# A graph layer on one core: fewer quads summed on TensorE, one-hot matrices ahead of the message product

## The chip, the cores and the metric

The kernel runs on one core of a Trainium2 chip. The core has four compute engines with a queue of instructions each: PE (TensorE, matrix products, with its weight loads in a row of their own, PEld), DVE (VectorE), ACT (ScalarE) and POOL (GpSimd). SP (SyncE) only issues DMAs here. The engines run side by side, each strictly in the order in which its instructions were written, and wait for each other by semaphores. The metric is the time of one execution in device microseconds (us), lower is better.

## The reference

6250 nodes with 128 features, 200000 edges. Each edge has a source and a target node (the edges come sorted by `dst`), 20 attributes and a weight. The layer normalises the node features, multiplies them by a matrix, makes a filter of 128 values for each edge from its attributes, multiplies the filter into the features of the edge's `dst` node, and sums the messages over the edge's `src` node, which is random:

```python
h = maximum(layernorm(x), 0)
xn = h @ W_in
W_ij = (softplus(f @ W_f1 + b_f1) - log 2) @ W_f2 + b_f2
W_ij = W_ij * edge_weight
out = segment_sum(xn[dst] * W_ij, src, 6250)
x + (softplus(out @ W_o1 + b_o1) - log 2) @ W_o2 + b_o2
```

All is in float32. The costly part is the sum into 6250 rows in random order.

## The kernel before

The edges are cut into chunks of 128 (one edge per partition), and four chunks make a quad: 391 quads. One loop (lines 1203 to 1248) has one pass, here called an item, per quad, and works on several quads at once, each one stage on: in item i the filter's first product `z` for quad i+1 (line 317) and its exponential and logarithm for quad i on ACT (322, 327); the gather of the node rows `xg` by a one-hot product (501) and the filter's second product `W` (509) for quad i-1; the scaling of `xg` by the edge weight on ACT into `xc` (514); and on DVE the message product, `W` times `xc` (524). `z`, `xg` and `W` share four PSUM banks in turn; a `z` takes the bank of the `W` three quads back, which the message product frees.

A quad's messages reach the sum in one of three ways, fixed by the quad's number:

- **Plain.** A product with an equality matrix sums the messages of a chunk that have the same source (536), and an indirect DMA from POOL adds the rows of the chunk to a table in DRAM (586): four scatters a quad, in item q+4. An equality matrix needs the sources broadcast to all partitions (loads at 348).
- **Listed.** Sixteen such quads make a window. Duplicated sources are found ahead of time (373 to 448), and get rows of their own in a list; the messages are scattered as they are, again four scatters a quad, in item q+2, and one more scatter a window adds the list. Of the plain and listed quads together 12 at the start and 19 at the end are plain.
- **Grouped.** The quad makes no scatter of its own. DVE builds a permutation matrix (`pm`, 665) that sorts the 512 edges into 16 groups of nodes with room for 32 edges each, and splits the message in a high part (ACT, 676) and a low or second part (DVE, 680) so that two passes of PE keep the precision. PE permutes (691, four outputs a quad), ACT copies the outputs out (696). Edges over 32 in a group go to a small overflow product (705, 706); two quads share one overflow, whose sums make one small scatter (`os`, `oji`). Eight grouped quads make a round. A round has four units, one for each of the permuted outputs: DVE builds a one-hot matrix for each quad (`so`, 768), PE multiplies (783, 64 products), DVE adds four PSUM banks to a sum in SBUF (794).

`sorted_quads` picks the grouped quads: it starts at `MP0` and steps by `MPGAPS`, over and over. Before, that is quad 2, then seven steps of 2 and one of 3: 8 of every 17 quads, 184 in all. `unit_slots` puts the units at offsets `UOFF` in that period.

The order of the rest is written out by hand. `at(item, point, function)` books a piece of work, and the loop runs the pieces of a point with `run`: `L` (loads, on SP), `D0` (first on DVE), `D1` (unit sums), `A0` and `A1` (on ACT ahead of the scaling), `DM` (DVE, just ahead of the message product), `PE2` (on PE behind the products of the item), `A2` (last on ACT), `D2` (last on DVE), `S` (scatters). `clear` moves a piece to a later item where a unit stands in its way. Node preparation (25 groups of 256 nodes, one every nine items: load, statistics, root, normalising, transpose, product, split in three parts, write of the table that `xg` is gathered from) and the split of the edge attributes run at such points too, so do the ranks in a group for eight quads at once (`rank_group` to `rank_slot`).

There are four tables for scatters. Two scatters into the same one must not overlap: the later one waits until the earlier one has landed. They are used in turn, the first two scatters into one table, then two, from the eighth three and from the 140th four. From a fixed scatter on one table gets no more and is added back within the loop (`r0_load`, `r0_tp`, `r0_add`).

Behind the loop all engines meet at a conditional loop (line 1277) that repairs rare cases and here does nothing. Then the tables are read (1360), added, and the output layer is computed in 13 groups.

The lines around the change in the loop:

```python
run(i, "A1")
if 0 <= i - 1 < NQ:
    s2_copy(i - 1)
run(i, "DM")
if 0 <= i - 1 < NQ:
    s2_m(i - 1)
```

Of the kernel before, what the change touches and what calls it, by code (L numbers as in the profile page):

```python
# [21 lines left out]
P = 128  # L22
# [15 lines left out]
LLATE = 16  # L38
# [16 lines left out]
def tile_gnn(ctx: ExitStack, tc: tile.TileContext, x, fB, cT, srcT, srcr, dstr, win_, wf1, wf2, bias, bo1c, wo1,  # L55
# [402 lines left out]
        mp["L", j] = {"so": idl[:, j:j + 1]}  # L458

    def l_dg(j):  # L460
        dg = wk.tile([P, P], F32, tag="h", name="ldg", bufs=1)
        nc.scalar.mul(dg, idt, idl[:, j:j + 1])
        mp["L", j]["dg"] = dg

    def l_same(j):
        eq = wk.tile([P, P], F32, tag="rm", name="leq", bufs=1)
# [371 lines left out]
    with tc.manual_schedule():  # L838
# [150 lines left out]
        for g in range(1, NG):  # L989
            if not spread:  # L990
                xt_load(g)
                for fn in (prep_stat, prep_rs0, prep_norm, prep_tp, prep_relu, prep_mm, prep_x1, prep_rm, prep_x2,
                           prep_x3):
                    fn(g)
                continue
            t0 = prep_start(g)
            at(t0 - 3, "L", xt_load, g)
            at(t0 - 1, "D2", prep_stat, g)
            at(t0, "A1", prep_rs0, g)
            at(t0, "D2", prep_norm, g)  # L1000
            at(t0 + 1, "PE2", prep_tp, g)
            at(t0 + 2, "A0", prep_relu, g)
            at(t0 + 2, "PE2", prep_mm, g)
            at(t0 + 3, "A0", prep_x1, g)
            at(t0 + 3, "DM", prep_rm, g)
            at(t0 + 3, "A2", prep_x2, g)
            at(t0 + 3, "D2", prep_x3, g)
        for b in range(1, NB):
            t0 = 2 if b == 1 else 8 * b - 8
            if b > 1:  # L1010
# [3 lines left out]
            at(t0 + 1, "A1", fb_3, b)  # L1014
            at(t0 + 1, "D2", fb_4, b)

        busy = units | {prep_start(g) + k for g in range(1, NG) for k in range(5)}
        mid = clear(NQ // 2, busy, 2) - 6 if spread else 0

        def late_loads():  # L1020
# [4 lines left out]

        def late_bias():
            nc.vector.tensor_scalar(nbo1, bo1_sb, -1.0, None, op0=ALU.mult)
            bb = wk.tile([P, 1, P], F32, tag="rm", name="bb", bufs=1)
# [6 lines left out]
            nc.vector.tensor_tensor(bo2b, bo2b, late["bps"][:, 0], op=ALU.add)  # L1035

        def bound_abs():
            t_ = wk.tile([K1, P], F32, tag="h", name="wabs", bufs=1)
            nc.scalar.activation(t_, w1f, AF.Abs)
            v_ = wk.tile([K1, P], F32, tag="rm", name="wsel", bufs=1)  # L1040
            nc.vector.tensor_copy(v_, con[:K1, 15:16].to_broadcast([K1, P]))
            late["wabs"] = t_, v_

# [62 lines left out]
            at(i, "PE2", r0_tp, g)  # L1106
            at(i + 1, "D0", r0_add, g)
        for r in range(-(-len(mpq) // RKQ)):
            i = max(mpq[RKQ * r], 5)
            at(i - 5, "D2", rank_group, r)  # L1110
            k = clear(i - 4, units)
            at(k, "PE2", rank_count, r)
            at(k + 1, "D0", rank_own, r)
            k = clear(k + 1, units)
            at(k, "PE2", rank_over, r)
            at(k + 1, "D0", rank_slot, r)
        for k in range(1, -(-NS // 2)):
            if not LB <= 2 * k < LE:
                at(max(0, splain[2 * k] - 2), "L", sb_load, k)
        for w in range((LE - LB) // SW):  # L1120
            for g in range(4):
                n = LB + SW * (w - 1) + 4 * g
                i = splain[n] + 2 if w else 6 + 2 * g
                for k in range(2):
                    kk = (LB + SW * w + 4 * g) // 2 + k
                    at(max(0, i + k - 2), "L", sb_load, kk)
                    at(i + k, "DM", l_eq, kk)
                i = clear(i + 2, units)
# [24 lines left out]
        if LE:  # L1153
            for k in range(NACC):
# [2 lines left out]
        for q in mpq:  # L1157
# [20 lines left out]
            if mpi[q] % 2 or q == mpq[-1]:  # L1178
                at(q + 5, "DM", over_idx, q)
                at(q + 6, "A0", over_dg, q)  # L1180
                k = clear(q + 6, units)
                at(k, "PE2", over_row, q)
                at(k + 1, "D0", over_eq, q)
                k = clear(q + 8, units)
# [15 lines left out]
        full = {-1: False}  # L1200
        r0_end = r0_at
        s1_pe(0)
        for i in range(max(NQ + 7, last + 16, r0_end + 2, lend + 24)):
            if i % 2 == 0 and i // 2 + 2 <= (NQ - 1) // 2:
                load_sc(i // 2 + 2)
            run(i, "L")
# [296 lines left out]
def base_caps(n, n_sc):  # L1503
    groups = node_groups(n)
    caps = []
    for s in range(n_sc):
        ready = n
        if big(n_sc) or s < 2:
            for g in range(1, len(groups)):
                if prep_start(g) + 3 >= 2 * s - 4:  # L1510
                    ready = groups[g][0]
                    break
        caps.append(ready - WIN)
# [86 lines left out]
```

## Time and profile before

| what | value |
|---|---|
| median of 3 runs | 2111.23 us (2109.82 to 2115.32) |
| profiled execution, its own time | 2102.09 us |
| its span | 2100.2 us |
| busy: PE, DVE, POOL, ACT | 85%, 84%, 76%, 73% |
| mean granted clock of PE | 0.93 |
| DMA | 269.16 MB, 128 GB/s |
| grouped quads, listed, plain | 184, 176, 31 |
| scatters of POOL: listed, plain, small | 704, 124, 103 |

The profiled execution is one run; its time stands 0.4% under the median of the three others. A row of a group gives the line, the engine, the operation, the output and the inputs, their shapes and the count; then the busy time in us and the mean length in ns; then the idle time that the engine had just ahead of these instructions and what ended it. A row of the waits gives who waited for whom, us in total, how often, and the longest. In a row by stretch stand the stretch, its length, the busy time of an engine with its count, the granted clock, the share of the DMA engines and GB/s.

### The profile page before, as it was taken

The page shows a single profiled execution, that of the slowest core. Times are in us where ns is not written, and L with a number is a line of the kernel's source. Part 1 is how long each engine was busy: PE and PEld are TensorE (multiplying, and loading weights), DVE is VectorE, ACT ScalarE, POOL GpSimd, SP SyncE. Part 2 cuts the span into 40 slices and gives each one's busy share as a digit, 9 for nine tenths or more (in the row PEclk, how much of TensorE's full clock was granted, in tenths as well). Part 3 has the DMA queues.
Part 4 walks back from the last instruction along what each step waited for, and adds up shares of the span by engine and source line. Part 5 has one row for each costly group of instructions (what it writes and reads, how often), then busy time and mean ns, then how long its engine had stood idle before and what let it go on. Part 6 is the DMA issues. An engine that isn't in the chain of part 4 may idle for free. (4 is left out here: it accounts for less than half of the span.)

```text
span 2100.2 us, 52738 instructions
## 1 busy us (share of the span) xinstructions
PE 1786.8 (85%) x17881; PEld 1532.4 (73%) x17881; DVE 1762.2 (84%) x4448; ACT 1537.2 (73%) x4392; POOL 1601.1 (76%) x984
## 2 busy tenths in 40 slices
PE   3579888887987898988988888888999899998966
PEld 2468777776776777877777777777777777887854
DVE  5687988898888898988989889798898888989865
ACT  3568777776776777777778687687877788898824
POOL 3557888786876877788787788788888888888844
PEclk9789999998999999989999999899999999999978
DMA  7886666665765666666676667666666666767649
GB/s 247 213 202 116 131 117 108 132 107 108 127 119 98 126 124 116 107 118 119 125 125 119 115 110 130 104 118 119 119 118 128 109 117 103 132 116 143 113 87 241
DMA packets 378865, 269.16 MB, mean 128 GB/s; under 512 B 96959, under 2 KB 342506, under 8 KB 378594
## 3 DMA queue, kind: packets, MB, share of 16 engines
q1 hardware_dynamic: 242642, 198.09, 33.7%
q0 software_dynamic: 135664, 67.63, 33.0%
q8 instruction: 141, 2.31, 0.5%
q14 instruction: 130, 1.06, 0.2%
q10 hardware_dynamic: 288, 0.07, 0.0%
HBM read 155.30 MB, written 110.31 MB: 126 GB/s over the span
## 5 line engine op out<-in xcount | busy, mean ns | idle before, releaser
L586 POOL DMA_INDIRECT acc<-s,lji x704 | 1180.3, 1677 | 297.3 <-issue 165.3
L514 ACT ACTIVATE xc<-xg,cb 128x128 f32<-128x128 f32 x1564 | 445.8, 369 | 94.3 <-PE xg L501 91.1
L691 PE MATMUL pq<-pt,pm 128*128 128x258 f32 x2944 | 471.6, 306 | 40.4 <-DVE pt L680 9.9
L509 PE MATMUL W<-w,a 128*128 128x128 f32 x3128 | 475.3, 297 | 0.0
L691 PEld LDWEIGHTS pq<-pt,pm 128*128 128x128 f32 x2944 | 401.6, 200 | 66.9 <-ACT mst L696 12.8
L509 PEld LDWEIGHTS W<-w,a 128*128 128x128 f32 x3128 | 398.4, 200 | 43.6 <-issue 5.9
L783 PE MATMUL un<-so,mst 32*128 32x392 f32 x5888 | 346.8, 368 | 60.9 <-DVE pr L630 40.0
L783 PEld LDWEIGHTS un<-so,mst 32*128 32x128 f32 x5888 | 294.1, 199 | 111.4 <-DVE pr L630 44.8
L665 DVE TENSOR_SCALAR pm<-iot,pos 128x576 fp32r<-128x576 f16 x736 | 345.1, 529 | 0.0
L696 ACT CAST mst<-pq 128x258 fp32r<-128x258 f32 x736 | 253.2, 373 | 113.5 <-PE pq L691 95.7
L327 ACT ACTIVATE a<-a,con 128x512 f32<-128x512 f32 x391 | 282.5, 723 | 12.8
L586 POOL DMA_INDIRECT acc<-s,ji x124 | 206.8, 1668 | 97.4 <-ACT ji L567 43.0
L768 DVE TENSOR_SCALAR so<-iot,mst 128x392 fp32r<-128x392 f16 x736 | 272.8, 431 | 1.4 <-PE un L783 1.4
L322 ACT ACTIVATE a<-z 128x512 f32<-128x512 f32 x391 | 236.3, 604 | 30.6 <-PE z L317 21.6
L794 DVE TENSOR_TENSOR accT<-un,accT 128x392 f32<-128x392 f32 x352 | 174.0, 555 | 35.1 <-PE un L783 34.7
L524 DVE TENSOR_TENSOR s<-W,xc 128x512 f32<-128x512 f32 x176 | 120.8, 687 | 95.0 <-ACT xc L514 87.5
L586 POOL DMA_INDIRECT acc<-os,oji x103 | 172.5, 1675 | 35.4 <-issue 17.7
L501 PE MATMUL xg<-wn,oh 63*128 63x128 bf16 x1564 | 160.2, 225 | 19.4 <-ACT xc L514 13.1
L705 PE MATMUL po<-pt,pm 128*64 128x130 f32 (+1 forms) x736 | 143.1, 251 | 37.7 <-ACT mst L696 24.0
L317 PE MATMUL z<-ft,ws 123*128 123x512 bf16 x391 | 154.3, 395 | 18.3 <-DMA ft<-fsd 15.3
L498 PE MATMUL W<-b2rep,onesb 64*128 64x512 bf16 x391 | 157.1, 402 | 0.0
L705 PEld LDWEIGHTS po<-pt,pm 128*64 128x64 f32 (+1 forms) x736 | 120.7, 168 | 47.2 <-ACT mst L696 29.8
(207 smaller groups left out, 2493.8 us busy)
## 6 DMA issues: line engine op xcount, KB each, us to landing
rb<-reld SPq DMA_DIRECT2D x391, 64.0 KB
fsd<-f SPq DMA_DIRECT2D x49, 480.0 KB
sb<-src SPq DMA_DIRECT2D x183, 128.0 KB
ft<-fsd SPq DMA_DIRECT2D x195, 120.0 KB
fb<-in_fB_dram SPq DMA_DIRECT2D x49, 320.0 KB
ft<-fsd SPq DMA_DIRECT2D x195, 80.0 KB
wn<-tab SPq DMA_DIRECT2D x782, 15.8 KB
acc<-s,lji POOLq DMA_INDIRECT x704
```

What stands on the lines that cost most here:

```text
L322: nc.scalar.activation(a, st[q]["z"], AF.Exp)
L327: nc.scalar.activation(a, a, AF.Ln, bias=half, scale=0.5)
L509: nc.tensor.matmul(W[:, c, :], st[q]["a"][:, c * P:(c + 1) * P], w2, start=False, stop=(c == 3))
L514: nc.scalar.mul(xc[:, c, :], st[q]["xg"][:, c, :], late["c", q // CQ][:, 4 * (q % CQ) + c:4 * (q % CQ) + c + 1])
L586: nc.gpsimd.indirect_dma_start(out=accs[k][:rows, :], out_offset=bass.IndirectOffsetOnAxis(ap=ji, axis=0), in_=s, in_offset=None, compute_ ...
L665: nc.vector.tensor_scalar(pm[:, c], iot[:, :SLOTS], rk[r]["pos"][:, 4 * j + c:4 * j + c + 1], None, op0=ALU.is_equal)
L691: nc.tensor.matmul(t[:, :PW], mp[q]["pm"][:, c, s * P:(s + 1) * P], pt[:, c], start=(c == 0), stop=(c == 3))
L696: nc.scalar.copy(mp[q]["ms", s], mp[q].pop(("q", s))[:, :PW])
L705: nc.tensor.matmul(o[:, :P + 2], w, pt[:, c, P:PW], start=(c == 0), stop=False)
L768: nc.vector.tensor_scalar(so, iotw[:, :GN], w[:, 2 * P:2 * P + 1], None, op0=ALU.is_equal)
L783: nc.tensor.matmul(ts[g][:, :GN], mp[q]["ms", s][v, k * P:(k + 1) * P], mp[q]["oh"][v], start=(q == qs[0] and k == 0), stop=(q == qs[-1] a ...
L794: nc.vector.tensor_tensor(v, t[:, :GN], v, op=ALU.add)
```

## The change

Three things change together. First the exchange: `MP0` is 8 and `MPGAPS` (2, 2, 2, 3), so that 4 of every 9 quads are grouped from quad 8 on: 168 quads, with two units in nine items (`UOFF` (2, 6)); the round of eight quads takes two periods. One more window of 16 quads is listed: 192 listed, 31 plain. The last grouped quad is 383 instead of 390.

Second the order on DVE: point `D2` (permutation matrices, second parts, half of the one-hots of a unit, node statistics and normalising, ranks, list ids, attribute pieces) moves from the end of the item to ahead of `DM` and the message product. The other half of a unit's one-hots keeps its place at the end, as a new point `D3`.

Third, small pieces move. The index of the overflow and of a list (`over_ji`, `l_ji`) is computed first on DVE in the next item and made an integer (`over_int`) on ACT ahead of the scaling, not within the item of its copy. Node preparation starts at two items picked by `calm`, which keeps off a unit's item and its neighbours; its last steps come an item or two later. The ranks of a round are computed up to some 20 items ahead, off the units. Some small tiles (`ldg`, `leq`, `bb`, `wabs`, `wsel`) get a tag of their own with three buffers, instead of the single buffers of `h` and `rm`.

```diff
-MP0 = 2
-MPGAPS = (2, 2, 2, 2, 2, 2, 2, 3)
+MP0 = 8
+MPGAPS = (2, 2, 2, 3)
-UOFF = (2, 6, 10, 14)
+UOFF = (2, 6)
...
-        dg = wk.tile([P, P], F32, tag="h", name="ldg", bufs=1)
+        dg = wk.tile([P, P], F32, tag="eql", name="ldg", bufs=3)
...
-            t0 = prep_start(g)
-            at(t0 - 3, "L", xt_load, g)
-            at(t0 - 1, "D2", prep_stat, g)
-            at(t0, "A1", prep_rs0, g)
-            at(t0, "D2", prep_norm, g)
-            at(t0 + 1, "PE2", prep_tp, g)
-            at(t0 + 2, "A0", prep_relu, g)
-            at(t0 + 2, "PE2", prep_mm, g)
-            at(t0 + 3, "A0", prep_x1, g)
-            at(t0 + 3, "DM", prep_rm, g)
-            at(t0 + 3, "A2", prep_x2, g)
-            at(t0 + 3, "D2", prep_x3, g)
+            t0, t1 = prep_start(g)
+            at(t0 - 5, "L", xt_load, g)
+            at(t0 - 2, "D2", prep_stat, g)
+            at(t0 - 1, "A1", prep_rs0, g)
+            at(t0 - 1, "D2", prep_norm, g)
+            at(t0, "PE2", prep_tp, g)
+            at(t0 + 1, "A0", prep_relu, g)
+            at(t1, "PE2", prep_mm, g)
+            at(t1 + 1, "A0", prep_x1, g)
+            at(t1 + 1, "DM", prep_rm, g)
+            at(t1 + 2, "A1", prep_x2, g)
+            at(t1 + 3, "D0", prep_x3, g)
...
-            i = max(mpq[RKQ * r], 5)
-            at(i - 5, "D2", rank_group, r)
-            k = clear(i - 4, units)
+            i = mpq[RKQ * r]
+            if i < 10:
+                k, o = i - 1, i
+            else:
+                k = max(k for k in range(i - 20, i - 4) if calm(k, units) == k and calm(k + 1, units) <= i)
+                o = calm(k + 1, units)
+            at(k - 1, "D2", rank_group, r)
             at(k, "PE2", rank_count, r)
             at(k + 1, "D0", rank_own, r)
...
-            at(k + 1, "DM", l_ji, w)
-            at(k + 1, "A2", over_int, ("L", w))
+            at(k + 2, "D0", l_ji, w)
+            at(k + 2, "A1", over_int, ("L", w))
             at(k + 2, "S", over_scatter, ("L", w))
...
-                at(k + 1, "DM", over_ji, q)
-                at(k + 1, "A2", over_int, q)
+                at(k + 2, "D0", over_ji, q)
+                at(k + 2, "A1", over_int, q)
                 at(k + 2, "S", over_scatter, q)
...
-                at(k - 2, "D2", unit_oh, r, s, 0)
+                at(k - 2, "D3", unit_oh, r, s, 0)
                 at(k - 1, "D2", unit_oh, r, s, 1)
...
+            run(i, "D2")
             run(i, "DM")
             if 0 <= i - 1 < NQ:
                 s2_m(i - 1)
...
             run(i, "A2")
-            run(i, "D2")
+            run(i, "D3")
...
+def calm(i, busy):
+    while i in busy or i + 1 in busy or i - 1 in busy:
+        i += 1
+    return i
...
 def prep_start(g):
     busy = unit_its(sorted_quads(4 * PREP_GAP * (g + 10)))
-    return clear(7 + PREP_GAP * (g - 1), busy, 3) - 1
+    t0 = calm(7 + PREP_GAP * (g - 1), busy)
+    return t0, calm(t0 + 1, busy)
```

More of the change, by code (lines that the diff above doesn't have):

```diff
@@ L465, in l_same @@
     def l_same(j):
-        eq = wk.tile([P, P], F32, tag="rm", name="leq", bufs=1)
+        eq = wk.tile([P, P], F32, tag="eql", name="leq", bufs=3)
         nc.vector.tensor_scalar(eq, mp["L", j].pop("row")[:, :P], idl[:, j:j + 1], None, op0=ALU.is_equal)
@@ L1015, in tile_gnn @@
             at(t0 + 1, "D2", fb_4, b)
-        busy = units | {prep_start(g) + k for g in range(1, NG) for k in range(5)}
+        busy = units | {t + k for g in range(1, NG) for t in prep_start(g) for k in range(2)}
         mid = clear(NQ // 2, busy, 2) - 6 if spread else 0
@@ L1027, in late_bias @@
             nc.vector.tensor_scalar(nbo1, bo1_sb, -1.0, None, op0=ALU.mult)
-            bb = wk.tile([P, 1, P], F32, tag="rm", name="bb", bufs=1)
+            bb = wk.tile([P, 1, P], F32, tag="eql", name="bb", bufs=3)
             nc.vector.tensor_copy(bb[:, 0], bo1_sb.to_broadcast([P, P]))
@@ L1037, in bound_abs @@
         def bound_abs():
-            t_ = wk.tile([K1, P], F32, tag="h", name="wabs", bufs=1)
+            t_ = wk.tile([K1, P], F32, tag="eql", name="wabs", bufs=3)
             nc.scalar.activation(t_, w1f, AF.Abs)
-            v_ = wk.tile([K1, P], F32, tag="rm", name="wsel", bufs=1)
+            v_ = wk.tile([K1, P], F32, tag="eql", name="wsel", bufs=3)
             nc.vector.tensor_copy(v_, con[:K1, 15:16].to_broadcast([K1, P]))
@@ L1108, in tile_gnn @@
         for r in range(-(-len(mpq) // RKQ)):
[L1109 to L1111 removed]
+            i = mpq[RKQ * r]
[5 more added lines that the diff above has]
+            at(k - 1, "D2", rank_group, r)
             at(k, "PE2", rank_count, r)
             at(k + 1, "D0", rank_own, r)
[L1114 to L1116 removed]
+            at(o, "PE2", rank_over, r)
+            at(o + 1, "D0", rank_slot, r)
         for k in range(1, -(-NS // 2)):
@@ L1127, in tile_gnn @@
                     at(i + k, "DM", l_eq, kk)
-                i = clear(i + 2, units)
+                i = calm(i + 2, units) if w and g < 3 else clear(i + 2, units)
                 at(i, "PE2", l_count, (LB + SW * w) // 4 + g)
@@ L1202, in tile_gnn @@
         s1_pe(0)
-        for i in range(max(NQ + 7, last + 16, r0_end + 2, lend + 24)):
+        for i in range(max(NQ + 7, last + 18, r0_end + 2, lend + 24)):
             if i % 2 == 0 and i // 2 + 2 <= (NQ - 1) // 2:
@@ L1509, in base_caps @@
             for g in range(1, len(groups)):
-                if prep_start(g) + 3 >= 2 * s - 4:
+                if prep_start(g)[1] + 3 >= 2 * s - 4:
                     ready = groups[g][0]
```

4 lines of the change are left out of this document (2 added, 2 removed).

## The prediction

> **What bounds the kernel now.** I read the page first, then all groups by line, the waits, and last the scatter line alone in seven stretches of the loop.
>
> ```profile
> span 2100.2 us, 52738 instructions
> PE 1786.8 (85%) x17881; PEld 1532.4 (73%) x17881; DVE 1762.2 (84%) x4448; ACT 1537.2 (73%) x4392; POOL 1601.1 (76%) x984
> L586 POOL DMA_INDIRECT acc<-s,lji x704 | 1180.3, 1677 | 297.3 <-issue 165.3
> L586 POOL DMA_INDIRECT acc<-s,ji x124 | 206.8, 1668 | 97.4 <-ACT ji L567 43.0
> L586 POOL DMA_INDIRECT acc<-os,oji x103 | 172.5, 1675 | 35.4 <-issue 17.7
> ```
>
> ```profile
> POOL acc L586 <- issue: 209.8, 686, 0.6
> POOL acc L586 <- DMA acc<-s,lji: 24.4, 62, 2.4
> POOL acc L586 <- DMA acc<-s,ji: 19.1, 17, 4.4
> POOL acc L586 <- DVE s L524: 68.7, 30, 6.4
> ```
>
> By the shares PE and DVE lead and POOL is third. That misleads: 686 of 931 scatters follow the one before after 209.8/686 = 0.306 us in which POOL waits for nothing. A scatter in a full queue therefore costs 1.677 + 0.306 = 1.983 us, and 931 of them 1846 us. The scatter line alone, by stretch (length, busy time, count):
>
> ```profile
> 52.00:242.00 190.00, 124.80 (x74) 0.85 0.73 167
> 242.00:490.00 248.00, 200.16 (x121) 0.93 0.68 121
> 490.00:950.00 460.00, 350.10 (x209) 0.93 0.64 115
> 950.00:1290.00 340.00, 270.57 (x163) 0.95 0.66 119
> 1290.00:1850.00 560.00, 469.99 (x279) 0.96 0.67 117
> 1850.00:2001.00 151.00, 124.06 (x76) 1.00 0.68 124
> 2001.00:2027.00 26.00, 20.05 (x12) 0.87 0.46 62
> ```
>
> Length minus busy minus 0.306 per scatter is what POOL really lacks: 42.6, 10.8, 45.9, 19.5, 4.6, 3.6 and 2.3 us, together 129; with the rows cut at the edges I use 131. From 1290 on POOL is full. Before, PE, DVE and ACT together (the chain that makes messages) are partly too slow for it. The same stretches for the exponential, one per item, give the item time:
>
> ```profile
> 490.00:950.00 460.00, 52.30 (x87) 0.93 0.64 115
> 950.00:1290.00 340.00, 41.68 (x69) 0.95 0.66 119
> 1290.00:1850.00 560.00, 72.71 (x120) 0.96 0.67 117
> ```
>
> That is 5.29, 4.93 and 4.67 us per item. The kernel has two bounds close together: POOL's queue, and in the middle the chain.
>
> The end, from the order of time:
>
> ```profile
> 58.55 1.82 POOL L586 DMA_INDIRECT acc<-s,ji  x1 [4.27 <-DMA acc<-s,ji]
> ...
> 2024.79 2.15 POOL L586 DMA_INDIRECT acc<-os,oji  x1 [2.66 <-DVE so L768]
> ...
> 2032.35 1.98 DVE L794 TENSOR_TENSOR accT<-un,accT 128x392 f32<-128x392 f32 x4 [3.26 <-PE un L783]
> ```
>
> All engines meet after the last evacuation (2034.3) and the last scatter (2026.9; it lands some 4.3 us later, an estimate from the wait of the second scatter on the first into the same sum). So POOL's end has 3.1 us to spare. The rest to 2100.2, 65.9 us, is untouched.
>
> **The exchange of quads.** By the schedule's own arithmetic 184 grouped quads become 168, and one more window of 16 quads is listed: 64 scatters more; the plain ones lose 1, the small ones go from 103 to 96. 931 become 987: 56 × 1.983 = +111 us for POOL. The other engines lose:
>
> ```profile
> L691 PE MATMUL pq<-pt,pm 128*128 128x258 f32 x2944 | 471.6, 306 | 40.4 <-DVE pt L680 9.9 <-ACT f L284 5.9 <-ACT mst L696 5.2
> L783 PE MATMUL un<-so,mst 32*128 32x392 f32 x5888 | 346.8, 368 | 60.9 <-DVE pr L630 40.0 <-DVE ldup L389 8.0 <-DVE so L768 6.4
> L665 DVE TENSOR_SCALAR pm<-iot,pos 128x576 fp32r<-128x576 f16 x736 | 345.1, 529 | 0.0
> L768 DVE TENSOR_SCALAR so<-iot,mst 128x392 fp32r<-128x392 f16 x736 | 272.8, 431 | 1.4 <-PE un L783 1.4
> L794 DVE TENSOR_TENSOR accT<-un,accT 128x392 f32<-128x392 f32 x352 | 174.0, 555 | 35.1 <-PE un L783 34.7
> L680 DVE TENSOR_TENSOR pt<-mb,pt 128x512 fp32r<-128x512 f32 x184 | 125.7, 683 | 0.0
> L373 DVE TENSOR_TENSOR eql<-sb,srcT_sb 128x1024 bf16<-128x1024 int16 x88 | 107.0, 1215 | 25.1 <-DMA sb<-src 21.0 <-PE xg L501 3.2 <-DMA ft<-fsd 0.9
> ```
>
> DVE: (345.1 + 272.8 + 174.0 + 125.7)/184 = 4.99 us a quad, less 107.0/176 = 0.61 for a listed one: 4.38 × 16 = 70 us, 0.18 an item. PE: at least (471.6 + 346.8)/184 × 16 = 71 us. One more window also brings eight loads of sources, four of lists, and their sum; the DMA engines are 0.64 to 0.68 busy in the loop's rows above, and the loads stand two items ahead. These gains count only where POOL starves.
>
> **Where the extra scatters fall.** With the first eight quads plain, 87 scatters are due before item 34 instead of 73: 14 × 1.98 = 27.8 us, inside a stretch that lacks 42.6. Some 13.9 of that is waiting for a scatter into the same sum to land (19.1 less 17 × 0.306); so about 2 us of hunger is left. From item 34 to 253 there are 544 instead of 522; those 22 fill 43.6 of the 76.2 us lacking from 242 to 1290. The other 32.6 go only if the chain gains 32.6/219 = 0.15 us an item there. Per item POOL will want (20 + 2 + 9/29)/9 = 2.48 scatters, 4.92 us, where 40.6/17 = 2.39 asked 4.73.
>
> **The moved one-hots and second parts.** On DVE they now stand ahead of the message product, which waits for ACT:
>
> ```profile
> DVE s L524 <- ACT xc L514: 87.5, 84, 3.8
> DVE m L524 <- ACT xc L514: 24.5, 16, 6.5
> DVE mb L524 <- ACT xc L514: 18.3, 23, 1.9
> ACT mst L696 <- PE pq L691: 95.7, 131, 5.5
> ACT oji L757 <- DVE ojd L753: 62.1, 41, 3.6
> DVE x L258 <- ACT x L252: 39.4, 15, 4.1
> ```
>
> The 130 us of waiting for the scaled rows cover them in part: a permutation matrix set takes 345.1/184 = 1.9 us, a second part 0.68. Work is only exchanged for idling. The price is a message later by what stands ahead; its scatter then starts later, which costs nothing while scatters queue. The edge pieces, node statistics, rank groups and list ids move with them; their two SP writes (pieces, table) wait less or the same, and loads behind them gain. From rows alone the move lies between −130 and, if every message comes 1.9 us later where POOL is dry (30 waits on messages, above), +57 us. I take 0.2 us an item gained, nearer the rows of waiting.
>
> **Small indices an item later.** ACT's 62.1 us wait for the index goes; behind it stood the next exponential. POOL's small scatter keeps its place at the end of the same item, so nothing is put behind it. Node preparation in two parts removes the 39.4 us. Its load is issued an item earlier and its table write up to two later, where SP waits for it as it does now; the reads of the table that need it lie items behind. One quad in four instead of three in eight has all its permutes in one item, where ACT copies wait on PE: 95.7 falls by about a third. Half of (62.1 + 39.4 + 32) over 391 items: 0.17. The new buffers cost no instruction; rank steps are fewer (21 for 23) and off POOL.
>
> So the chain gains about 0.18 + 0.2 + 0.17 = 0.55 us an item at best, 0.35 if these overlap: more than the 0.15 needed. 5.29 becomes 4.9, which is POOL's own pace. I leave 3 us of hunger there and 4 later.
>
> **Length of a scatter.**
>
> ```profile
> L586 POOL DMA_INDIRECT acc<-s,lji x704: 1541/1554/2935, 194.8 to 1844.9; - x176
> ```
>
> The mean of 1677 is 123 ns over the median. One-hot work per scatter falls to (168/184)/(987/931) = 0.86; if all the excess came from it, 17 ns go, if none, 0. I take 10 ns: 987 × 0.010 = −10 us. The Trainium skill, "SBUF — State Buffer", section "Who interferes with whom", says that a VectorE instruction in a two-port mode shuts GpSimd out of a shared port for its whole length. By that rule the whole 17 ns would go, −17 us, and the total would be 7 us lower; no row quoted here isolates it.
>
> **Sum.** POOL's last scatter: +111 − 10 − (131 − 28) = −2. The 28 are 19 for landings (24.4 + 19.1 less 79 × 0.306) and 2 + 3 + 4. It ends at 2024.9 and has landed at 2029.2. PE and DVE do not set the end then: the last unit comes seven items earlier (395 for 402), so the row at 2032.35 moves forward. The meeting moves from 2034.3 to 2029.2: −5. The profiled run took 2102.1 us; the three runs have a median of 2111.2, 9 more. Against the median: 2106.
>
> **Rivals.**
>
> ```profile
> L317 PE MATMUL z<-ft,ws 123*128 123x512 bf16 x391 | 154.3, 395 | 18.3 <-DMA ft<-fsd 15.3 <-ACT a L322 2.0 <-DVE s L524 1.0
> ```
>
> *The chain does not gain (slower).* Messages behind 1.9 us of one-hots free their PSUM late; the next z waits, and what ACT and DVE saved returns. The group of z shows hardly any such wait now (the row's last number), which speaks against; the chain's slow middle at 5.29 speaks for. Then 32.6 of hunger and 4 more stay, S = 28 + 30 = 58, and scatters do not shorten: +111 − (131 − 58) = +38, less the 3 to spare: +35, 2146. It decides from a gain under 0.13 us an item on; every 0.1 less costs 22 us.
> *POOL never starves, one-hots were its brake (faster).* S = 19 and 17 ns: −5 − 9 − 7, 2090. For: the stretch after 1290 lacks only 4.6 of 560. Against: the dry moments in the middle come in bursts.
> *Nothing moves to speak of:* 2111, where both meet halfway; it lies between the first two.
>
> **Numbers.** Forecast 0.45, slower rival 0.35, faster rival 0.20. A difference under 0.3%, 6 us, cannot be told from none. The forecast's own range is 2094 to 2120; of its 0.45 I give 0.22 to faster, 0.15 to the same, 0.08 to slower. With the rivals: faster 0.42, same 0.17, slower 0.41 (0.02 of the slow rival lies within). The range reaches 2084 to 2146.
>
> **What would show it.** Scatters 987, their mean near 1.67, POOL's lack about 28 us, the last scatter near 2025; item time of 4.9 between 490 and 950; the three waits ACT oji, DVE x and DVE s much smaller. Wrong: item time above 5 there with POOL waiting on messages; or PE's z waiting on DVE; or a first stretch slowed by DMA, whose share is already 0.73.

## The result, and the profile after

The changed kernel takes 2168.27 us (median of 4 runs, 2159.82 to 2171.44) where the kernel before takes 2111.32 on the same chip (four runs; the table further up has three of them): a ratio of 1.026, 95% interval 1.0225 to 1.0296. It is slower; the forecast was 2106. The profiled execution took 2171.36 us, 0.14% over the median.

The page of the changed kernel, its span and its engines:

```profile
span 2168.5 us, 50733 instructions
PE 1741.5 (80%) x17021; PEld 1511.4 (70%) x17021; DVE 1705.5 (79%) x4259; ACT 1492.1 (69%) x4251; POOL 1682.6 (78%) x1040
```

PE lost 45 us of work, DVE 57, ACT 45, as grouped quads went; POOL gained 82. Yet all of PE, DVE and ACT are idle for longer than before. The scatter line by stretch (length, POOL's busy time and count, clock, DMA share, GB/s):

```profile
52.00:242.00 190.00, 134.34 (x81) 0.82 0.79 178
242.00:490.00 248.00, 206.08 (x124) 0.89 0.65 115
490.00:950.00 460.00, 351.07 (x213) 0.88 0.64 115
950.00:1290.00 340.00, 263.26 (x159) 0.89 0.64 115
1290.00:1850.00 560.00, 470.68 (x283) 0.92 0.66 117
```

Length less busy less 0.306 a scatter, as in the prediction: POOL lacks 30.9, 4.0, 43.8, 28.1 and 2.7 us. From 490 to 950 it is as hungry as before (45.9), from 950 to 1290 more so (19.5). That is 109.5 us in sum (108 over the whole loop, counted gap by gap), where the prediction left 28. The exponential, one per item, in two of these stretches:

```profile
490.00:950.00 460.00, 52.45 (x86) 0.88 0.64 115
950.00:1290.00 340.00, 39.09 (x64) 0.89 0.64 115
```

5.35 and 5.31 us an item, where 5.29 and 4.93 stood and 4.9 was forecast. The chain, with 16 grouped quads less to do, has become slower. In the waits (total, times, longest) the three that were to go did not all go, and others are there instead:

```profile
DVE pt L680 <- ACT pt L676: 100.4, 81, 4.7
ACT pt L676 <- DVE mb L524: 93.2, 42, 6.2
...
DVE s L524 <- ACT xc L514: 90.1, 100, 4.4
PEld po L705 <- ACT mst L696: 70.3, 26, 4.9
ACT dg L725 <- DVE ovs L720: 65.5, 31, 5.2
```

ACT's wait for the small index is down from 62.1 to 5.0 and DVE's for the node rows (39.4) is gone; DVE's for the scaled rows (87.5) is not. New is ACT waiting for a grouped quad's message (`mb`) ahead of its high part, and DVE waiting for that high part. The group of the high part, before and then after (the last numbers are idle time just ahead of it):

```profile
L676 ACT CAST pt<-mb 128x512 fp32r<-128x512 f32 x184 | 114.0, 620 | 0.9 <-DVE mb L524 0.6
```

```profile
L676 ACT CAST pt<-mb 128x512 fp32r<-128x512 f32 x168 | 104.2, 620 | 121.7 <-DVE mb L524 93.2 <-DVE eql L373 15.0 <-DVE so L768 7.6
```

From 0.9 us to 121.7. One such moment in the order of time (start, length, engine and line, in brackets the idle time before and who ended it):

```profile
545.62 0.18 DVE L597 CAST srcf<-srcT_sb 128x32 f32<-128x32 int16 x1
...
546.15 1.16 PE L509 MATMUL W<-w,a 128*128 128x128 f32 x8
546.22 0.63 ACT L696 CAST mst<-pq 128x258 fp32r<-128x258 f32 x2
...
547.98 1.80 DVE L665 TENSOR_SCALAR pm<-iot,pos 128x576 fp32r<-128x576 f16 x4
...
549.69 0.69 DVE L524 TENSOR_TENSOR mb<-W,xc 128x512 f32<-128x512 f32 x1
...
550.41 0.62 ACT L676 CAST pt<-mb 128x512 fp32r<-128x512 f32 x1 [3.56 <-DVE mb L524]
...
551.04 1.14 ACT L514 ACTIVATE xc<-xg,cb 128x128 f32<-128x128 f32 x4
551.07 0.69 DVE L680 TENSOR_TENSOR pt<-mb,pt 128x512 fp32r<-128x512 f32 x1 [0.69 <-ACT pt L676]
...
552.21 0.69 DVE L524 TENSOR_TENSOR s<-W,xc 128x512 f32<-128x512 f32 x1 [0.45 <-ACT xc L514]
...
553.32 0.36 ACT L696 CAST mst<-pq 128x258 fp32r<-128x258 f32 x1
...
553.73 0.56 PE L691 MATMUL pq<-pt,pm 128*128 128x258 f32 x2 [4.47 <-ACT mst L696]
```

`W` was there at 547.31. DVE was then at a rank group and at the one-hots of this very quad, and made the message at 549.69, some 2.4 us later. ACT, which had nothing more to do ahead of its high part, stood still for 3.56 us. Behind the high part on ACT stand the scaling of the next quad's rows and the copies out of the permuted rows: so DVE waits for the scaling, and PE 4.47 us for the copy that frees a bank. One delayed message has stopped three engines. The rank group's 2.4 us have a share in this moment: without them the message would have started at about 547.3, just as `W` was there. Of the 42 waits of ACT for a grouped message, 16 (52.7 us) have a rank group in the 6 us ahead of them and 26 (40.5 us) have not; which of the moved pieces costs the time is therefore a matter for the experiments. In the changed order the one-hots of quad q stand directly ahead of the message product of the same quad q (both in item q+1), and ACT's high part is booked in item q+2 *ahead* of the scaling.

### The profile page after: what moved, and what is told of

Same layout as the page of the kernel before. It is cut to its first block, busy times and chain, and to the rows that moved or that the text cites. A ratio compares the mean times of both kernels' runs of the same rounds, so it can differ in the third digit from the quotient of the medians.

```text
span 2168.5 us, 50733 instructions
## 1 busy us (share of the span) xinstructions
PE 1741.5 (80%) x17021; PEld 1511.4 (70%) x17021; DVE 1705.5 (79%) x4259; ACT 1492.1 (69%) x4251; POOL 1682.6 (78%) x1040
## 5 line engine op out<-in xcount | busy, mean ns | idle before, releaser
L586 POOL DMA_INDIRECT acc<-s,lji x768 | 1275.2, 1660 | 312.3 <-issue 184.6
L509 PE MATMUL W<-w,a 128*128 128x128 f32 x3128 | 504.9, 310 | 0.0
L509 PEld LDWEIGHTS W<-w,a 128*128 128x128 f32 x3128 | 425.4, 211 | 46.5 <-issue 12.3
L665 DVE TENSOR_SCALAR pm<-iot,pos 128x576 fp32r<-128x576 f16 x672 | 314.3, 529 | 1.2 <-PE pq L691 0.9
L696 ACT CAST mst<-pq 128x258 fp32r<-128x258 f32 x672 | 227.1, 372 | 120.6 <-PE pq L691 90.2
L783 PE MATMUL un<-so,mst 32*128 32x392 f32 x5376 | 277.5, 350 | 13.9 <-ACT s L544 9.6
L783 PEld LDWEIGHTS un<-so,mst 32*128 32x128 f32 x5376 | 246.7, 188 | 45.1 <-issue 19.1
L768 DVE TENSOR_SCALAR so<-iot,mst 128x392 fp32r<-128x392 f16 x672 | 249.6, 431 | 13.7 <-PE un L783 12.3
L524 DVE TENSOR_TENSOR s<-W,xc 128x512 f32<-128x512 f32 x192 | 132.4, 690 | 122.1 <-ACT xc L514 90.1
L680 DVE TENSOR_TENSOR pt<-mb,pt 128x512 fp32r<-128x512 f32 x168 | 116.1, 691 | 124.8 <-ACT pt L676 100.4
L676 ACT CAST pt<-mb 128x512 fp32r<-128x512 f32 x168 | 104.2, 620 | 121.7 <-DVE mb L524 93.2
```

The source lines that it names most:

```text
L509: nc.tensor.matmul(W[:, c, :], st[q]["a"][:, c * P:(c + 1) * P], w2, start=False, stop=(c == 3))
L586: nc.gpsimd.indirect_dma_start(out=accs[k][:rows, :], out_offset=bass.IndirectOffsetOnAxis(ap=ji, axis=0), in_=s, in_offset=None, compute_ ...
L665: nc.vector.tensor_scalar(pm[:, c], iot[:, :SLOTS], rk[r]["pos"][:, 4 * j + c:4 * j + c + 1], None, op0=ALU.is_equal)
L696: nc.scalar.copy(mp[q]["ms", s], mp[q].pop(("q", s))[:, :PW])
L768: nc.vector.tensor_scalar(so, iotw[:, :GN], w[:, 2 * P:2 * P + 1], None, op0=ALU.is_equal)
L783: nc.tensor.matmul(ts[g][:, :GN], mp[q]["ms", s][v, k * P:(k + 1) * P], mp[q]["oh"][v], start=(q == qs[0] and k == 0), stop=(q == qs[-1] a ...
```

## The experiments

The kernel before ran beside each set on the same chip (medians 2107.0 to 2111.3); ratios are to those runs, with 95% intervals.

### The parts alone and undone

**The exchange of quads alone** (e1), on the kernel before:

```diff
-MP0 = 2
-MPGAPS = (2, 2, 2, 2, 2, 2, 2, 3)
+MP0 = 8
+MPGAPS = (2, 2, 2, 3)
-UOFF = (2, 6, 10, 14)
+UOFF = (2, 6)
```

> The kernel before with the exchange of quads alone (4 of 9 from quad 8), the order on DVE and all small pieces as before. Order theory (the new order makes DVE and ACT wait for each other within an item, and that cancels the gain of the exchange): scatters 987, the chain faster than before by some 0.15 us an item, POOL full for longer, 2100 to 2125 us. Quad theory (56 scatters more in a full queue are the whole loss): near the changed kernel, 2150 to 2175 us, with POOL lacking about as much as before.

Measured: 2098.68 us, ratio 0.9943 (0.9917 to 0.9969), a little under the range of the first theory. POOL lacks only 32 us over the loop here: the exchange by itself takes nearly all of its hunger away.

**The order alone** (e2), on the kernel before (`D2` ahead of the message; the two pieces that stay late, `prep_x3` and the first `unit_oh`, go to the old place, now `D3`):

```diff
+            run(i, "D2")
             run(i, "DM")
             if 0 <= i - 1 < NQ:
                 s2_m(i - 1)
...
-            run(i, "D2")
+            run(i, "D3")
```

> The kernel before with the new order alone: one-hots, second parts and the rest of their point ahead of the message product (the last step of node preparation stays at the end of the item). Order theory: slower than before by 30 to 60 us, 2140 to 2170, with DVE waiting at the second part for ACT's high part and ACT at the high part for the message, some 90 us each, and items of 5.4 us or more between 490 and 950 us. Quad theory: no loss, 2095 to 2115.

Measured: 2128.70 us, 1.0081 (1.0058 to 1.0105). The order alone makes the kernel slower, but by less than either bound of the first theory; the other, no loss, is missed too.

**The order back** (e3), in the changed kernel (`D2` behind the message again; quads and third part as changed):

> The changed kernel with the old order on DVE (that point back behind the message product), all else changed. Order theory: the two waits go to about nothing, items between 490 and 950 us fall from 5.35 to 5.0 or less, 2105 to 2130 us. Quad theory: within 10 us of the changed kernel, 2158 to 2178.

Measured: 2094.07 us, 0.991 (0.9882 to 0.9939). It is faster than the changed kernel and than the one before, and the fastest of all kernels with every scatter, though its interval overlaps that of e1. It is also faster than was expected. Its scatter line in two stretches, and its high part:

```profile
490.00:950.00 460.00, 389.52 (x232) 0.91 0.68 122
950.00:1290.00 340.00, 287.54 (x173) 0.95 0.70 125
```

```profile
L676 ACT CAST pt<-mb 128x512 fp32r<-128x512 f32 x168 | 104.2, 620 | 4.9 <-DVE mb L524 4.7
```

POOL lacks nothing in either stretch (460 - 389.52 - 232 x 0.306 is -0.5), over the whole loop 29 us, and its last scatter ends at 2032.0: near the prediction's sum for POOL (lack 28, end 2024.9), in the kernel without the order. The order costs 74 us in all, far more than the gain that was expected.

**Only the second parts back** (e4; `part_lo` from `D2` to `D3`):

> The changed kernel with the second parts alone back at the end of the item; the one-hots stay ahead of the message. Order theory, if the loss is the hand-over message, high part, second part: DVE's wait for the high part (100 us) goes, 2115 to 2145 us. If it is the length of all that stands ahead of the message: within 15 us of the changed kernel. Quad theory: 2158 to 2178.

Measured: 2197.19 us, 1.0403 (1.0369 to 1.0438), slower still and outside all three ranges. DVE's wait for ACT's high part is not what costs: without it DVE waits 274.0 us for the scaling of listed quads, where the changed kernel had 90.1. Why that costs 29 us more was not followed up.

### What in the order costs

**ACT's high part later** (e5): behind the scaling and the copies, and the second part an item later:

```diff
-            at(q + 2, "A1", part_hi, q)
-            at(q + 2, "A1", part_ext, q)
-            at(q + 2, "D2", part_lo, q)
+            at(q + 2, "A2", part_hi, q)
+            at(q + 2, "A2", part_ext, q)
+            at(q + 3, "D0", part_lo, q)
```

> The changed kernel, with ACT's high part and its tail moved to the end of ACT's item (behind the scaling of the next rows and the copies of the permuted rows) and DVE's low part to the start of the next item. The one-hots and second parts stay ahead of the message product. Theory of the lost slack (the message product now ends only 0.26 us ahead of the point where ACT takes its high part; ACT waits for it there, and what stands behind, the scaling and the copies, is late for DVE and PE): nothing on ACT stands behind that wait any more, so the idle time ACT pt <- DVE mb (93.2) and DVE pt <- ACT pt (100.4) nearly goes, and the time falls to 2090 to 2115. Rival of length (the message product itself comes later by what stands ahead of it on DVE, and the item is as long as that): the hand-over is no matter, 2150 to 2175.

Measured: 2124.32 us, 1.0086 (1.0048 to 1.0125): 44 of the 74 us are back, less than expected; the time lies between the two ranges. The wait itself is smaller but still there:

```profile
ACT pt L676 <- DVE mb L524: 64.5, 38, 5.7
```

**Only the one-hots back** (e6; `perm_oh` and the second `unit_oh` from `D2` to `D3`):

> The changed kernel with the permutation one-hots and the one-hots of the small units behind the message product again; everything else of the moved group (second parts, edge pieces, node statistics, rank groups) stays ahead. Theory of the lost slack, and the rival of length: the 1.9 us sets of one-hots are nearly all of the work that delays the message, so 2095 to 2120. Rival of a wait inside the group (a moved second part or edge piece waits itself for ACT in the same item, and holds the message behind it): unchanged, 2150 or more.

Measured: 2108.37 us, 1.0003 (0.9981 to 1.0026). 60 of the 74 us are back. The rest of the group (second parts, edge pieces, statistics, rank groups) costs the other 14. ACT still waits 34.1 us for grouped messages, and 32.3 of these have a rank group in the 6 us ahead of them.

**Only the one-hots ahead** (e7), the rest of the group behind the message:

> The changed kernel with only the permutation one-hots and the one-hots of the small units ahead of the message product; the rest of the moved group behind it as before the change. Theory of the lost slack and rival of length: most of the loss stays, 2140 to 2170. Rival of a wait inside the group: the loss goes with the second parts and edge pieces, 2095 to 2110.

Measured: 2169.52 us, 1.0291 (1.0249 to 1.0333): as slow as the whole. Two of its waits:

```profile
DVE s L524 <- ACT xc L514: 259.7, 140, 7.9
...
ACT pt L676 <- DVE mb L524: 75.7, 65, 2.5
```

Here DVE no longer waits for the high part, since its second part stands behind the message; it waits for the scaling instead, which stands behind the same high part on ACT. The wait has only changed its name. With e6 this puts most of the loss on the one-hots, and rules out a wait inside the rest of the group.

**The same one-hots, an item later** (e9). Grouped quads are two or three apart, so in item q+2 the message product behind the one-hots of quad q is never that of a grouped quad:

```diff
-            at(q + 1, "D2", perm_oh, q)
+            at(q + 2, "D2", perm_oh, q)
```

> The changed kernel with the permutation one-hots of a grouped quad an item later, still ahead of the message product: the product they now delay is that of the next quad, which is never a grouped one and has no hand-over to ACT's high part; the grouped quad's own product keeps its old place. All that stands ahead of message products is as long as in the changed kernel. Theory of the lost slack: the hand-over gets its 1.9 us back, ACT pt <- DVE mb (93.2 in the changed kernel, 2 or none before) falls under 30, and the time is 2090 to 2115. Rival of length (any product behind 1.9 us of one-hots is late for POOL and for PE, grouped or not): unchanged, 2150 to 2175. Between them: both.

Measured: 2104.18 us, 0.9956 (0.9937 to 0.9975). As much work stands ahead of message products as in the changed kernel, and 64 of the 74 us are back.

```profile
L676 ACT CAST pt<-mb 128x512 fp32r<-128x512 f32 x168 | 104.2, 620 | 51.6 <-DVE mb L524 32.3 <-DVE ext L610 7.5 <-DVE ltwo L436 4.2
```

So what costs is not that a message comes later, but that a *grouped* quad's message does, the one that ACT takes ahead of its scaling. This edit also has DVE come 1.9 us later to the second part, so that it waits less for ACT; but e7, where that wait is gone altogether, is no faster, so this is not the reason.

### The third part alone

The changed kernel with the old quads and the old order: what is left (e8) is the small indices an item later, node preparation in two parts, the rank steps, the buffers.

> The kernel before with only the third part of the change: small indices, their entries and sums an item later, node preparation in two parts, rank steps moved, the new buffers; quads 8 of 17 from 2 and the old order of DVE's item. The prediction counted 0.17 us an item for it. e3 (order back) took 2094.1 and e1 (quads alone) 2098.7, a difference of 4.6. If that is this part's gain, about 2100 to 2104; if the part is worth nothing by itself where 40.6 us of grouping an item are asked of the chain, 2105 to 2110; if it frees the full 0.17 an item where POOL starves (about 219 items), 2075 to 2090.

Measured: 2115.12 us, 1.0028 (1.0007 to 1.0049). No gain; if anything a loss, and above the range for "worth nothing". The wait that this part was to remove has grown, from 62.1 us:

```profile
ACT oji L757 <- DVE ojd L753: 93.7, 61, 5.2
```

### The chain by itself

Three kernels (e10 before, e11 changed, e12 changed with the old order) in which POOL issues only two of the four scatters of a listed quad, so that it is never full (the result lacks the other messages of these quads):

```diff
             for c in range(nchunks(q)):
+                if c >= 2:
+                    sc_n[0] += 1
+                    continue
                 scatter(st[q]["m"][:, c, :P],
```

> The kernel before, with only two of the four scatters of each listed quad issued (the output lacks the other half of these quads), so that POOL is far from full and the item time is the chain's own pace: the disputed term measured by itself. The prediction takes the chain as the limit at 5.29 us an item between 490 and 950 us and says that the change gives it 0.35 to 0.55. If that reading of the middle is right, this kernel has about 5.0 to 5.3 us an item from 490 to 1850; if the 5.29 was POOL's hunger and fullness by turns, about 4.6.

> The changed kernel with the same two of four scatters of each listed quad left out. The prediction: 0.35 to 0.55 us an item less than the run beside it with the kernel before. Theory of the lost slack: not less but 0.1 to 0.4 more; a lower granted clock as in the changed kernel (0.89) may come with it. Rival that POOL is part of it (messages late only because their buffers come free late): as fast as the run beside it with the old order.

> The changed kernel with the old order of DVE's item and the same two of four scatters left out. Beside the same cut of the kernel before this gives the exchange and the third part on the chain alone: the prediction counts 0.18 + 0.17 us an item less. Beside the same cut of the changed kernel it gives the price of the order by itself: the prediction says the order gives 0.2 us, the theory of the lost slack that it costs 0.3 to 0.5.

Measured: 2086.57, 2158.01 and 2033.89 us (one run each). The exponential by stretch, in this order:

```profile
490.00:950.00 460.00, 53.06 (x88) 0.93 0.48 102
950.00:1290.00 340.00, 41.73 (x69) 0.97 0.51 106
1290.00:1850.00 560.00, 74.16 (x122) 0.97 0.52 105
```

```profile
490.00:950.00 460.00, 52.97 (x87) 0.89 0.48 101
950.00:1290.00 340.00, 39.60 (x65) 0.89 0.50 104
1290.00:1850.00 560.00, 70.64 (x116) 0.92 0.50 102
```

```profile
490.00:950.00 460.00, 58.24 (x95) 0.95 0.54 111
950.00:1290.00 340.00, 43.55 (x71) 0.93 0.53 110
1290.00:1850.00 560.00, 74.67 (x122) 0.96 0.54 109
```

Item times of the chain alone: before 5.23, 4.93 and 4.59 us; changed 5.29, 5.23, 4.83; changed with the old order 4.84, 4.79, 4.59. Three things follow. The reading of the middle was right: the kernel before is chain-bound there, and nearly as slow with half of POOL's work gone. In the third stretch, where POOL was full, the chain alone is only 0.08 us an item faster (4.59 for 4.67): the two bounds lie close there. The changed kernel hardly depends on POOL at all: with 384 of 987 scatters left out it is 10 us faster. And the order by itself costs the chain 2158.0 - 2033.9 = 124 us, 0.32 an item, while exchange and third part together give it 2086.6 - 2033.9 = 52.7 us, 0.13 an item on the mean of all items and 0.39 and 0.14 in the two stretches where POOL starved.

### Where the order is dear

The order on top of each of the other parts. **Order and third part, old quads** (e13):

> The changed kernel with the old quads (8 of 17 from 2): order and third part together, without the exchange. Alone the order took 2128.7 (before 2107.0) and the third part 2115.1 (before 2107.3). If the two only add up: 2130 to 2145. If the third part is what makes the order dear (its sums and indices now stand at ACT's point ahead of the scaling, behind the same wait): 2165 to 2200. If the exchange is what makes it dear: as in the sum, or less.

Measured: 2237.11 us, 1.0577 (1.0546 to 1.0608), dearer than all three expectations.

**Order and quads, old third part** (e14):

> The kernel before with the new quads (4 of 9 from 8) and the order, without the third part. The quads alone took 2098.7, nearly POOL's own pace; on the chain alone exchange and third part gave 52.5 us. If the order's price here is the 45 us it has on the kernel before, the chain ends no later than POOL's queue: 2095 to 2115. If the exchange makes the order dear (124 us on the chain): 2145 to 2180.

Measured: 2163.97 us, 1.0236 (1.0207 to 1.0264). Then in both the permutation one-hots an item later, the edit of e9 (e17, e18):

> Order and third part with the old quads (2237.1), the permutation one-hots an item later, still ahead of message products. If the grouped quad's own product is all of it here too: the third part alone took 2115.1, so 2115 to 2135. If the third part brings a second wait (the index of the overflow rows, ACT dg <- DVE ovs, 146.2 in that run, whose DVE step also stands behind the moved group): 2150 to 2200. Unchanged, 2225 or more: the mechanism found on the whole change is not that of this case.

> Order and quads with the old third part (2164.0), the permutation one-hots an item later, still ahead of message products. If the grouped quad's own product is all of it: the quads alone took 2098.7, so 2098 to 2115. If not: 2140 or more.

Measured: 2117.66 us, 1.0057 (1.0035 to 1.0078), and 2110.64 us, 1.001 (0.9993 to 1.0027). All of it together, ratios to the kernel before:

| quads and third part | old order | order of the change | that, one-hots an item later |
|---|---|---|---|
| neither | 1 | 1.0081 | not run |
| new quads | 0.9943 | 1.0236 | 1.0010 |
| third part | 1.0028 | 1.0577 | 1.0057 |
| both | 0.9910 | 1.0260 | 0.9956 |

The order costs 22, 65, 122 and 74 us by rows (differences of medians; by the ratios 17, 62, 116 and 74); one edit, which takes the grouped quad's own product from behind its one-hots, gives back 53 of 65, 119 of 122 and 64 of 74 (by the ratios 48, 110 and 64). So one mechanism makes most of the loss in all three. Why it is small on the kernel before and largest with the third part is not settled. With the old third part the order brings another wait as well: PE's `z` waits 25.8 us for the message product in e2 and 7.4 in e14, where it is 1.0 before and 1.2 in the changed kernel. In e13 ACT's wait for the overflow index, whose DVE step is booked ahead of the message too, is more than double that of the changed kernel:

```profile
DVE pt L680 <- ACT pt L676: 148.6, 97, 4.5
...
ACT dg L725 <- DVE ovs L720: 146.2, 59, 5.7
```

It fell to 73.8 with the one-hots moved. That fits one engine's delay handed to the other and back, but no run takes this wait away alone.

### A version between

If 16 quads of grouping are worth 111 us of POOL and, with the third part, 52.7 of the chain, 8 quads might do better. Quads 8 of 17 from quad 8 on give 176 grouped quads, once with the third part and the old order (e15), once (e16) as the only edit on the kernel before (`MP0 = 8`).

> The changed kernel with the old order and quads 8 of 17 from quad 8 on: 176 grouped quads and by the schedule 958 scatters, between the 931 of before and the 987 of the change. POOL against the run with the order back (2094.1): 29 x 1.98 = 57 us less, 2037 if it never starved more. The chain: 2033.9 with 168 quads, and for 8 more half of the 52.5 us that 16 gave, 2060. Meeting with some hunger of POOL: 2060 to 2080. If the middle starves as in the kernel before, 2085 to 2100.

> The kernel before with only the first grouped quad at 8 instead of 2, everything else as before: 176 grouped quads, 958 scatters. Chain: 2086.6 with 184 quads, half of the 52.5 us less, 2060; POOL as in the run beside it, 2037. 2060 to 2085; if the third part has a gain of its own, some 5 more than the run beside it.

Measured: 2136.07 us, 1.0108 (1.0078 to 1.0137), and 2119.67 us, 1.0035 (1.0017 to 1.0053): both missed. The scatter line of the second and its exponential in one stretch:

```profile
490.00:950.00 460.00, 359.45 (x218) 0.95 0.65 119
```

```profile
490.00:950.00 460.00, 54.35 (x90) 0.95 0.65 119
```

5.11 us an item, and POOL lacks 460 - 359.45 - 218 x 0.306 = 33.8 us there. The expectation took the gain by the count of quads. But the period is still 8 of 17, so in the middle as many quads an item are grouped as before; the 8 quads fewer lie at the ends, where the chain does not limit, and 27 more scatters come on top. What frees the chain is the density in the stretch that it limits, 4 of 9 against 8 of 17. e16 and e1 differ only in it and in the places of the units that go with it, and over the whole loop POOL lacks 109 us in e16 and 32 in e1. The third part does not help at this density either: e15, which has it, is 16 us slower than e16, with intervals that do not overlap.

## Why the prediction was wrong, and where it was right

- **What bounds the kernel: right.** The chain limits the middle (5.23 us an item with half of POOL's work gone, 5.29 with all). POOL limits the rest, but by little: 4.67 us an item from 1290 to 1850, where the chain alone needs 4.59.
- **The exchange and POOL's sum: right, but the gain came from elsewhere.** 987 scatters; from one profile to the other their mean fell by 12.6 ns (10 was taken; with the order back only 6). With the order back POOL lacks 29 us for 28, and PE and DVE have 64 and 68 us less to do (71 and 70 were taken; in the changed kernel 45 and 57). But POOL's last scatter then ends at 2032.0 and in e1 at 2037.6, not ahead of the 2026.9 of before. In these profiles both kernels are faster only because what follows the last scatter takes 60.7 and 59.5 us instead of 73.3, and the sum had put that part down as untouched. By the medians they gain 13 and 8 us, which the 12.6 and 13.7 us saved there account for. So a time near the forecast would have been partly luck.
- **The moved one-hots and second parts: the step that failed.** The prediction counted "0.2 us an item gained"; on the chain alone it is 0.32 lost. Its sentence was: "The price is a message later by what stands ahead; its scatter then starts later, which costs nothing while scatters queue." That is true of the quads that scatter, but a grouped quad makes no scatter of its own. Its message goes to ACT, whose queue has the scaling behind it, on which DVE's next message waits, and the copies, on which PE waits. The 130 us of waiting for scaled rows were read as room for other work on DVE. They were the far end of a loop between two engines, and work put ahead of the message lengthened the loop: 98 of the 130 us stayed (90.1 for listed quads), and ACT's 93.2 us and DVE's 100.4 came beside them. The bound of +57 us from above was too low too, since it priced only POOL's waits for messages.
- **Small indices: over-sized.** 0.17 us an item was taken. In the changed kernel ACT's and DVE's waits went as said (62.1 to 5.0; 39.4 gone), but ACT's went only with the order: with the order back it is 41.4, in the third part alone 93.7. The new place puts the index and its use in one item, where ACT can wait for DVE's first piece as it waited before. The third part alone gains nothing (1.0028), at 176 grouped quads it loses (e15 against e16), and on the new quads it may gain: 0.991 against 0.9943, intervals that overlap. Together with the exchange 0.35 was taken; the chain alone shows 0.39 and 0.14 in the two starved stretches, 0.13 over all items.
- **The slower rival: right in sign, wrong in mechanism.** It had PE's `z` waiting for a bank that a late message frees. That wait is 1.2 us in the changed kernel, 1.0 before; it shows only in kernels with the order and the old third part (25.8 us in e2). Its 2146 was still 22 short.
- **POOL's end and after.** The last scatter ended 82.0 us later than before: 56 scatters +111, their length -12.4, hunger -23, a first scatter at 59.2 instead of 52.6 us +6.6. The rest was said to be untouched, without a reason beyond that; it became shorter, 59.6 us from the last scatter's end to the end of the span where it was 73.3. It goes by the quads alone: 59.3 to 61.7 us in all twelve kernels with 4 of 9 grouped, 70.7 to 74.0 in the six that have 8 of 17 from quad 2. The reads of the tables began 17.0 us behind the last scatter's end before, and 5.2 after:

```profile
2037.24 6.67 SPq L1255 DMA_DIRECT2D xr<-in_x_dram  x10
...
2043.95 8.51 SPq L1360 DMA_DIRECT2D ta_in<-acc  x10
```

```profile
2107.38 1.54 POOL L586 DMA_INDIRECT acc<-os,oji  x1 [0.30 <-issue]
...
2114.10 6.08 SPq L1364 DMA_DIRECT2D ta_in<-acc  x9
```

In the changed kernel PE and DVE are done with the loop ahead of POOL. The 13 loads for the output layer, ten of which stood on SP's queue straight ahead of the table reads before, are all issued by 2093.6, and ten of the 13 additions run beside POOL's last scatters instead of behind them. That the reads start sooner for this reason was not tested by a run of its own.

- **A lower clock does not account for it.** The granted clock fell from 0.932 to 0.891, but the profiled runs of e9 and e6 have 0.899 and 0.901 at 2116 and 2109 us, and that of e14 0.905 at 2164.

## What to carry to other kernels

Before work is put ahead of a step that "has slack", list everyone who takes that step's result, and what stands behind the taker in its own queue; here the taker that mattered was not the one that bounds the kernel. Idle time on an engine in front of a wait is no free room if the engine it waits for is waiting, one item back, for this one. And a gain by counts (fewer grouped quads) counts only at the density of the stretch that is limited: measure that stretch by itself, with the other bound cut away, before adding items up.

## What the hardware showed that was not expected

In the changed kernel one scatter near the end took 6.93 us instead of 1.54. It started inside a run of ten additions on DVE whose two inputs both lie in SBUF. The same in the kernel with the order back:

```profile
2092.15 6.08 DVE L1262 TENSOR_TENSOR xr<-xr,bo2b 128x512 f32<-128x512 f32 x10
2092.73 6.93 POOL L586 DMA_INDIRECT acc<-s,ji  x1 [0.31 <-issue]
```

```profile
2015.25 6.09 DVE L1262 TENSOR_TENSOR xr<-xr,bo2b 128x512 f32<-128x512 f32 x10
...
2016.57 6.19 POOL L586 DMA_INDIRECT acc<-s,ji  x1 [0.30 <-issue]
```

The additions end at 2098.23 and 2021.34, the scatters at 2099.66 and 2022.76: 1.43 and 1.42 us later, wherever in the run they began. In all twelve kernels with such a run, these two among them, it is 1.41 to 1.43. The scatter does nearly all of its work after the last addition, as if POOL were shut out of something for the whole run. The Trainium skill, "SBUF — State Buffer", section "Who interferes with whom", says that a VectorE instruction with two SBUF inputs contends with a GpSimd instruction that reads SBUF, and that the second to issue is blocked for the whole instruction; these rows agree, if the scatter's reading of its indices counts as such a read, which no run separates. The same place infers that descriptor generation does not suffer from such additions; these scatters were held all the same. Some 5 us of POOL's queue go there, in a stretch that sets the end; no run moved the additions.
